# Moving the zeroing of one accumulator, grouping two more quads, and shifting two small steps in a graph-convolution kernel

## The chip, the cores and the metric

The kernel runs on one core of one Trainium2 chip. The metric is the device time of one execution in microseconds (us); before the change it was 2064.23 us, the median of three runs (2063.2 to 2068.42). A profiled execution of the same kernel took 2063.64 us.

## What is computed

A message-passing layer on 6250 nodes and 200000 edges, with the edges sorted by `dst`:

```python
h = jnp.maximum(_layernorm(x, axis=-1), 0.0)
xw = h @ W_in
W_ij = (shifted_softplus(f_ij @ W_f1 + b_f1) @ W_f2 + b_f2) * f_ij_cutoff
x_ij = xw[dst] * W_ij                          # one row of 128 for each edge
out = segment_sum(x_ij, src, num_segments=6250)
x = x + shifted_softplus(out @ W_o1 + b_o1) @ W_o2 + b_o2
```

The sum over `src`, which is in no order, is the hard part: every edge's row of 128 floats must be added to the row of its source node.

## The kernel before

**Chunks, quads and items.** 128 edges are a chunk and four chunks a quad; there are 1563 chunks and 391 quads. One long loop (`tile_gnn`, under `manual_schedule`) runs over items i = 0 to 398; item i starts the first matmul of quad i+1, the softplus of quad i, the second matmul of quad i-1, and so on. Whatever does not belong to every item is hung on a point of an item with `at(item, point, function)`. The points of one item follow each other in this order: L (loads), D0 and D1 (VectorE), A0 and A1 (ScalarE), DM and DR (VectorE), PE1 and PE2 (TensorE), A2 (ScalarE), D2 (VectorE), S (scatters). Each engine executes its own instructions in the order in which they were recorded, and so does each queue of DMA issues, SyncE's (SP) for all plain loads and stores in the loop and GpSimd's (POOL) for the scatters.

**How a quad's rows reach the sum.** There are two ways.

- A *plain* or *listed* quad is scattered: after pre-summing duplicates (plain: an equality matrix `eq` and four matmuls into `pp`, L547, copied to `s` by ScalarE, L555; listed: a list of duplicates worked out ahead) four indirect DMAs, one for each chunk, add its rows to an accumulator in DRAM (`scatter`, L597). There are four accumulators `acc0` to `acc3`, which the scatters take in turn: the first 140 scatters use three of them, later ones all four, and the last 64 leave out `acc0`, which is then read back (`r0_load`, `r0_tp`, `r0_add`, L1097) into the on-chip accumulator `accT`. A scatter waits until the one before it on the same accumulator has landed. The tile `s` has four buffers; each comes free when the scatters that read it have landed.
- A *grouped* quad is not scattered. A one-hot matrix `pm` (L677) permutes its rows by node group into 512 slots and 64 overflow slots; 16 matmuls (`pq`, L702) and 4 copies (L708) make four tiles `mst`. Eight grouped quads are a round. For each round four *units* (`unit_oh`, `unit_pe`, `unit_evac`) build one-hot matrices `so` (L780), multiply them with `mst` in 8 x 3 x 4 = 96 small matmuls into four PSUM banks `un` (L795), and add these to `accT` (L806). Overflow rows of two grouped quads share one scatter (`over_pe` to `over_scatter`, L715, L722, L742 to L769, index `oji`).

`sorted_quads` picks the grouped quads: from 8 on with gaps 2, 2, 2, 3, up to quad 390, cut to whole rounds. That gives 168 quads, the last one 383, in 21 rounds, and leaves 223 quads to be scattered, of which 192 are listed. All in all there are 987 scatters. `unit_slots` puts the last round's units on items 389, 391, 393 and 395; the last scatter, the overflow of quads 381 and 383, is due in item 394.

**Ranks.** Where a node's rows go in a permutation is worked out for eight quads at once: `rank_group` (VectorE, point D2, six items ahead of the round's first quad) makes the group one-hot `G` (L608 to L614) and then the counts and offsets `cnt`, `loc`, `ext` (L616 to L622); `rank_count` (TensorE, next item) uses `G`, `rank_own` and `rank_slot` the rest.

**Zeroing.** The accumulators are zeroed in ten DMAs of 320 KB each, from the first 640 columns of `accT`, which are set to zero at the start. `acc0` and `acc1` are zeroed through POOL's queue; `zero_piece` (L168) does `acc2` in items 0 to 4 and `acc3` in items 5, 7, ... 23 through SP's queue, between the loads.

**End.** Behind the loop a flag is read by all engines (would the rare slow path be needed? it is not taken with these inputs), all engines meet there, and the last stage begins: it loads `acc1` to `acc3` (L1378), adds them to `accT` and applies the last two matmuls, 13 groups of up to 512 nodes.

PSUM has four banks for all of `pp`, `pq`, `po`, `un`, `rtp` and other small results (tag B), and four for `z`, `xg` and `W`.

Of the kernel before, what the change touches and what calls it, by code (L numbers as in the profile page):

```python
# [26 lines left out]
SLOTS = GRP * CAP + OVC  # L27
MP0 = 8
MPGAPS = (2, 2, 2, 3)
MPEND = 0  # L30
RND = 8
EXTRA = 0
RKQ = 8
UOFF = (2, 6)
SW = 16
# [19 lines left out]
def tile_gnn(ctx: ExitStack, tc: tile.TileContext, x, fB, cT, srcT, srcr, dstr, win_, wf1, wf2, bias, bo1c, wo1,  # L55
# [3 lines left out]
    NP = x.shape[0]  # L59
# [15 lines left out]
    ACC_R = NP + P  # L75
    GN = NP // GRP
    ZR = 10 if ACC_R % 10 == 0 else 1
    ZL = 3
    K1_END, K2_END, K3_END = 2, 8, 140
    Z2, Z3 = [0,0,1,1,2,2,3,3,4,4], [5+2*j for j in range(10)]  # L80
    mpq = sorted_quads(NQ)
    mpi = {q: n for n, q in enumerate(mpq)}
    units = unit_its(mpq)
# [54 lines left out]
    wo1_sb = cp.tile([P, P], F32, name="wo1_sb")  # L138
    wo2_sb = cp.tile([P, P], F32, name="wo2_sb")
    accT = cp.tile([P, NP], F32, name="accT")  # L140
    zero = accT[:, :ACC_R // ZR]
    wgtb = cp.tile([P, 1], BF16, name="wgtb")
    iotw = cp.tile([P, GN // 2 + SLOTS], F16, name="iot")
    iot = iotw[:, GN // 2:]
# [455 lines left out]
    rk = {}  # L600
    mp = {}

    def rank_group(r):
        qs = mpq[RKQ * r:RKQ * r + RKQ]
        nc4 = 4 * len(qs)
        srcf = wk.tile([P, 4 * RKQ], F32, tag="srcf", name="srcf", bufs=1)
        o = 4 * (NS + RKQ * r)
        nc.vector.tensor_copy(srcf[:, :nc4], srcT_sb[:, o:o + nc4])  # L608
        srcf = srcf[:, :nc4]
        n = [P, nc4, GRP - 1]  # L610
        nc.vector.tensor_tensor(ge[:, :nc4, 1:GRP], srcf.unsqueeze(2).to_broadcast(n),
                                thr.unsqueeze(1).to_broadcast(n), op=ALU.is_ge)
        G = wk.tile([P, 4 * RKQ, GRP], BF16, tag="G", name="G", bufs=1)
        nc.vector.tensor_tensor(G[:, :nc4], ge[:, :nc4, :GRP], ge[:, :nc4, 1:], op=ALU.subtract)  # L614
        cnt = wk.tile([P, 4 * RKQ], F32, tag="cnt", name="cnt", bufs=1)
        nc.vector.tensor_reduce(cnt[:, :nc4], ge[:, :nc4, 1:GRP], axis=AX.X, op=ALU.add)  # L616
        loc = wk.tile([P, 4 * RKQ], F32, tag="loc", name="loc", bufs=1)
        nc.vector.scalar_tensor_tensor(loc[:, :nc4], cnt[:, :nc4], float(-GN), srcf, op0=ALU.mult, op1=ALU.add)
        ext = wk.tile([P, 4 * RKQ, 3], BF16, tag="ext", name="ext")
        nc.vector.memset(ext[:, :, 0], 0.0)  # L620
        nc.vector.tensor_scalar(ext[:, :nc4, 1], loc[:, :nc4], float(-(GN // 2)), None, op0=ALU.add)
        nc.vector.tensor_copy(ext[:, :nc4, 2], cnt[:, :nc4])  # L622
        rk[r] = {"G": G[:, :nc4], "cnt": cnt[:, :nc4], "ext": ext, "n": nc4, "qs": qs}

    def before_me(ps_t, src, w):
        n = src.shape[1]
# [79 lines left out]
    def perm_out(q, s):  # L706
        mp[q]["ms", s] = wk.tile([P, MW], BF16, tag=f"ms{s}", name="mst", bufs=RND + max(EXTRA, 2 * s))
        nc.scalar.copy(mp[q]["ms", s][:, :PW], mp[q].pop(("q", s))[:, :PW])  # L708
# [66 lines left out]
    def unit_oh(r, s, h):  # L775
        qs = round_quads(mpq, r)
        for q in qs[:len(qs) // 2] if h == 0 else qs[len(qs) // 2:]:
            so = wk.tile([P, GN], BF16, tag="so", name="so", bufs=RND + EXTRA)
            w = mp[q]["ms", s].bitcast(F32)
# [70 lines left out]
    with tc.manual_schedule():  # L850
# [26 lines left out]
        ext = cp.tile([HALF, 6], F32, name="ext")  # L877
# [86 lines left out]
        def at(i, point, fn, *a):  # L964
            hooks.setdefault((i, point), []).append((fn, a))
# [6 lines left out]
        if CE < EP // P:  # L972
            w = (CE + 4 * NS) // 2
# [131 lines left out]
        if spread:  # L1105
            k = clear(mid + 9, busy, 2)
# [3 lines left out]
            k = clear(NQ - 1, busy, 2)  # L1110
# [11 lines left out]
        for t in range(0, NPT, 4):  # L1122
            i = mid + 8 * (t // 4) if spread else 0
            at(min(i + 9, NQ + 1), "D2", x_bias, t)
        r0_at = 0
        for g in range(len(tgroups)):
            i = clear(max(r0_at + 1, ret_at + 5), units)
# [4 lines left out]
        for r in range(-(-len(mpq) // RKQ)):  # L1132
            i = mpq[RKQ * r]
            i = max(i, 6)
            at(i - 6, "D2", rank_group, r)
            at(i - 5, "PE2", rank_count, r)
            at(i - 4, "D0", rank_own, r)
            k = mpq[RKQ * r] if i == 6 else i - 2
            at(k, "PE2", rank_over, r)
            at(k + 1, "D0", rank_slot, r)  # L1140
# [3 lines left out]
        for w in range((LE - LB) // SW):  # L1144
            for g in range(4):
                n = LB + SW * (w - 1) + 4 * g
                i = splain[n] + 2 if w else 6 + 2 * g
                while w and (i - MP0) % sum(MPGAPS) not in UOFF:
                    i -= 1
                for k in range(2):  # L1150
                    kk = (LB + SW * w + 4 * g) // 2 + k
                    at(max(0, i + k - 2), "L", sb_load, kk)
                    at(i + k, "DM", l_eq, kk)
                i = clear(i + 2, units)
                at(i, "PE2", l_count, (LB + SW * w) // 4 + g)
                at(i + 1, "D0", l_dup, w, g)
            i += 1
            at(i, "D0", l_scan, w)
            i = clear(i, units)
            at(i, "PE2", l_before, w)  # L1160
            at(i + 1, "D0", l_index, w)
            assert i + 1 <= splain[LB + SW * w] + 1
            at(i + 2, "D2", l_id, w)
            i = clear(i + 3, units)
            at(i, "PE2", l_place, w)
            at(i + 1, "D0", l_take, w)
            i = clear(wend[w] + 12, units)
            at(i, "L", l_start, w)
            at(i, "A0", l_dg, w)
            at(i, "PE2", over_row, ("L", w))  # L1170
            at(i + 1, "D0", l_same, w)
            k = clear(i + 1, units)
            at(k - 1, "L", l_load, w)
            at(k, "PE2", l_sum, w)
            at(k + 1, "A0", l_copy, w)
            at(k + 1, "DM", l_ji, w)
            at(k + 1, "A2", over_int, ("L", w))
            at(k + 2, "S", over_scatter, ("L", w))
        if LE:
            for k in range(NACC):  # L1180
# [2 lines left out]
        for q in mpq:  # L1183
            at(q + 1, "D2", perm_oh, q)
            at(q + 2, "DR", part_rem, q, 1)
            at(q + 2, "DR", part_rem, q, 2)
            at(q + 2, "A2", part_ext, q)
            if q + 4 in units:
                for s in range(4):
                    at(q + 3, "PE2", permute, q, s)  # L1190
                for s in range(4):
                    at(q + 3, "PE2", perm_out, q, s)
            else:
                for s in range(4):
                    at(q + 3 + s // 2, "PE2", permute, q, s)
                    at(q + 4 + s // 2, "A0", perm_out, q, s)
            if mpi[q] % 2 or q == mpq[-1]:
                k = mpq[mpi[q] + 1] + 1 if mpi[q] + 1 < len(mpq) else q + 3
                at(k, "PE1", over_pe, q)
                at(k, "PE1", over_out, q)  # L1200
                at(q + 5, "DM", over_idx, q)
                at(q + 6, "A0", over_dg, q)
                k = clear(q + 6, units)
                at(k, "PE2", over_row, q)
                at(k + 1, "D0", over_eq, q)
                k = clear(q + 8, units)
                at(k, "PE2", over_sum, q)
                at(k + 1, "A0", over_copy, q)
                at(k + 1, "DM", over_ji, q)
                at(k + 1, "A2", over_int, q)  # L1210
                at(k + 2, "S", over_scatter, q)
        last = mpq[-1]
        for r in range(len(mpq) // RND):
# [263 lines left out]
def sorted_quads(nq):  # L1477
    qs, q = [], MP0
    while q < nq - MPEND:
        qs.append(q)  # L1480
        q += MPGAPS[(len(qs) - 1) % len(MPGAPS)]
    return qs if len(qs) % RND <= EXTRA else qs[:len(qs) // RND * RND]

# [23 lines left out]
def clear(i, busy, n=1):  # L1507
    while any(i + k in busy for k in range(n)):
        i += 1
    return i  # L1510
# [113 lines left out]
```

## Time and profile before

| | us |
|---|---|
| median of 3 runs (lowest, highest) | 2064.23 (2063.2, 2068.42) |
| profiled execution | 2063.64 |
| its span, first to last instruction | 2061.9 |
| TensorE (PE) busy | 1820.4 |
| GpSimd (POOL) busy | 1652.4 |
| VectorE (DVE) busy | 1650.9 |
| ScalarE (ACT) busy | 1470.8 |

The profile is of one execution. Times within it are counted from the first instruction. A line of the timeline gives start, duration, engine, line of the code, operation, tiles (out<-in) and count, and in brackets how long the engine was idle ahead of it and what ended that. A line of the table of stages gives the stretch, then busy time and count of each engine (or of one line alone), the granted TensorE clock, the busy share of the DMA engines and GB/s. In the groups of instructions, the numbers behind the first bar are busy time in us and mean duration of one in ns, and behind the second the idle time of the engine ahead of them.

### The profile page before, as it was taken

To read this page: it belongs to the slowest core of one execution; us is meant where nothing else is said; L and a number is where in the kernel's file an instruction comes from. 1 tells how busy PE (TensorE), PEld (TensorE's weight loads), DVE (VectorE), ACT (ScalarE), POOL (GpSimd) and SP (SyncE) were. 2 spreads that over 40 slices of the span, in tenths; PEclk is the share of its full clock that TensorE was granted. 3 is DMA by queue.
4 is the path that set the end of the run, shared out by engine and by line. 5 is a ranking of instruction groups with operands and counts; after the bars stand their busy time and mean duration, and the time that the engine had idled before them with its cause. 6 is when DMAs were issued, how large, how long until landed. Compare 5 with 4: busy or idle time off the path is not lost.

```text
span 2061.9 us, 54889 instructions
## 1 busy us (share of the span) xinstructions
PE 1820.4 (88%) x19121; PEld 1188.1 (58%) x19121; DVE 1650.9 (80%) x4449; ACT 1470.8 (71%) x3999; POOL 1652.4 (80%) x1040
## 2 busy tenths in 40 slices
PE   2578998899999999899989999999799899999966
PEld 1455555556655665565656566566565556666734
DVE  3577897798987988888888989888788687787745
ACT  2458776777777787777778787787677677788714
POOL 3578887888888888878788888888888888888884
PEclk9789999999999999999999999999999999999987
DMA  6887766667676776667666666766666666667647
GB/s 240 242 202 141 129 123 123 111 111 144 118 136 120 128 136 111 130 115 131 129 121 125 121 126 117 126 117 132 113 116 114 125 105 118 108 119 141 128 44 250
DMA packets 359675, 272.41 MB, mean 132 GB/s; under 512 B 97727, under 2 KB 319850, under 8 KB 359394
## 3 DMA queue, kind: packets, MB, share of 16 engines
q0 software_dynamic: 143728, 71.30, 34.4%
q1 hardware_dynamic: 215378, 197.50, 32.8%
q8 instruction: 151, 2.47, 0.5%
q14 instruction: 130, 1.06, 0.2%
q10 hardware_dynamic: 288, 0.07, 0.0%
HBM read 154.45 MB, written 114.24 MB: 130 GB/s over the span
## 4 chain that ended last, share of the span: by engine, by line
PE 46%; DVE 20%; ACT 10%; DMA 7%; issue 6%; POOL 5%; SPq 4%; DVEq 0%; ACTq 0%; POOLq 0%
PE pq L702 15%; PE W L520 10%; PE un L795 8%; POOL acc L597 5%; ACT xc L525 3%; PE po L715 2%; DVE accT L806 2%; DVE pt L691 2%; PE z L328 2%; ACT mst L708 2%; DVE eql L384 2%; PE xg L512 2%; DMA acc<-s,lji 2%; DVE pm L677 2%; ACT a L333 2%
## 5 line engine op out<-in xcount | busy, mean ns | idle before, releaser
L597 POOL DMA_INDIRECT acc<-s,lji x768 | 1254.4, 1633 | 250.4 <-issue 185.5
L702 PE MATMUL pq<-pt,pm 128*128 128x387 bf16 x2688 | 545.6, 346 | 43.2 <-ACT pt L697 10.6
L525 ACT ACTIVATE xc<-xg,cb 128x128 f32<-128x128 f32 x1564 | 448.0, 377 | 80.5 <-PE xg L512 73.4
L520 PE MATMUL W<-w,a 128*128 128x128 f32 x3128 | 467.7, 294 | 0.0
L520 PEld LDWEIGHTS W<-w,a 128*128 128x128 f32 x3128 | 392.2, 197 | 42.9 <-issue 4.5
L708 ACT CAST mst<-pq 128x387 bf16<-128x387 f32 x672 | 305.4, 481 | 149.7 <-PE pq L702 108.7
L702 PEld LDWEIGHTS <-pm 128*128 128x128 bf16 x2688 | 261.1, 100 | 235.6 <-issue 60.9
L795 PE MATMUL un<-so,mst 32*128 32x392 bf16 x8064 | 372.5, 327 | 11.9 <-ACT s L555 5.8
L795 PEld LDWEIGHTS <-mst 32*128 32x128 bf16 x8064 | 226.1, 93 | 152.0 <-issue 45.3
L338 ACT ACTIVATE a<-a,con 128x512 f32<-128x512 f32 x391 | 282.3, 722 | 12.7
L597 POOL DMA_INDIRECT acc<-s,ji x123 | 198.4, 1613 | 80.1 <-issue 26.7
L333 ACT ACTIVATE a<-z 128x512 f32<-128x512 f32 x391 | 238.0, 609 | 30.5 <-PE z L328 20.1
L691 DVE TENSOR_TENSOR pt<-pt 128x512 f32<-128x512 f32 x336 | 231.6, 689 | 5.8
L535 DVE TENSOR_TENSOR pt<-W,xc 128x512 f32<-128x512 f32 x168 | 115.5, 687 | 132.4 <-PE po L715 62.9
L677 DVE TENSOR_SCALAR pm<-iot,pos 128x576 bf16<-128x576 f16 x672 | 219.8, 388 | 0.0
L535 DVE TENSOR_TENSOR s<-W,xc 128x512 f32<-128x512 f32 x192 | 131.8, 686 | 75.7 <-ACT xc L525 44.6
L780 DVE TENSOR_SCALAR so<-iot,mst 128x392 bf16<-128x392 f16 x672 | 181.2, 333 | 9.7 <-PE un L795 9.2
L597 POOL DMA_INDIRECT acc<-os,oji x96 | 158.1, 1647 | 30.4 <-issue 18.3
L806 DVE TENSOR_TENSOR accT<-un,accT 128x392 f32<-128x392 f32 x320 | 158.4, 557 | 28.6 <-PE un L795 18.9
L512 PE MATMUL xg<-wn,oh 63*128 63x128 bf16 x1564 | 158.9, 224 | 25.0 <-DVE oh L345 13.8
L328 PE MATMUL z<-ft,ws 123*128 123x512 bf16 x391 | 151.7, 388 | 15.5 <-POOL b2rep L942 9.3
L509 PE MATMUL W<-b2rep,onesb 64*128 64x512 bf16 x391 | 155.6, 398 | 0.2 <-issue 0.2
(210 smaller groups left out, 1968.1 us busy)
## 6 DMA issues: line engine op xcount, KB each, us to landing
rb<-reld SPq DMA_DIRECT2D x391, 64.0 KB
fsd<-f SPq DMA_DIRECT2D x49, 480.0 KB
ft<-fsd SPq DMA_DIRECT2D x195, 120.0 KB
sb<-src SPq DMA_DIRECT2D x169, 128.0 KB
fb<-in_fB_dram SPq DMA_DIRECT2D x49, 320.0 KB
ft<-fsd SPq DMA_DIRECT2D x195, 80.0 KB
wn<-tab SPq DMA_DIRECT2D x782, 15.8 KB
acc<-s,lji POOLq DMA_INDIRECT x768
```

The source lines that it names most:

```text
L333: nc.scalar.activation(a, st[q]["z"], AF.Exp)
L338: nc.scalar.activation(a, a, AF.Ln, bias=half, scale=0.5)
L512: nc.tensor.matmul(xg[:, c, :], st[q]["oh"][a:a + NR, c * P:(c + 1) * P], wn[a:a + NR, c // 2, :], start=True, stop=True)
L520: nc.tensor.matmul(W[:, c, :], st[q]["a"][:, c * P:(c + 1) * P], w2, start=False, stop=(c == 3))
L525: nc.scalar.mul(xc[:, c, :], st[q]["xg"][:, c, :], late["c", q // CQ][:, 4 * (q % CQ) + c:4 * (q % CQ) + c + 1])
L535: nc.vector.tensor_tensor(m[:, :, :P], st[q]["W"], st[q]["xc"], op=ALU.mult)
L597: nc.gpsimd.indirect_dma_start(out=accs[k][:rows, :], out_offset=bass.IndirectOffsetOnAxis(ap=ji, axis=0), in_=s, in_offset=None, compute_ ...
L677: nc.vector.tensor_scalar(pm[:, c], iot[:, :SLOTS], rk[r]["pos"][:, 4 * j + c:4 * j + c + 1], None, op0=ALU.is_equal)
L691: nc.vector.tensor_tensor(pt[:, :, k * P:(k + 1) * P], a, high(a), op=ALU.subtract)
L702: nc.tensor.matmul(t[:, :PW], mp[q]["pm"][:, c, s * P:(s + 1) * P], high(mp[q]["pt"][:, c:c + 1, :PW])[:, 0], start=(c == 0), stop=(c == 3))
L708: nc.scalar.copy(mp[q]["ms", s][:, :PW], mp[q].pop(("q", s))[:, :PW])
L795: nc.tensor.matmul(ts[g][:, :GN], mp[q]["ms", s][v, k * P:(k + 1) * P], mp[q]["oh"][v], start=(q == qs[0] and k == 0), stop=(q == qs[-1] a ...
```

## The change

Four things change at once. `acc3` is zeroed in items 13, 16, ... 40, from the last 640 columns of `accT` (those of the first, which are overwritten earlier, could not serve so long). The list of grouped quads may run to 389 and may leave up to two quads over, which join the last round: quads 386 and 388 are now grouped, the last round has ten quads, the `so` tile ten buffers and the first `mst` tile ten, and the last units stand in items 394, 396, 398 and 400. The conversion of the overflow scatter's index to integers (`over_int`) moves from the end of ScalarE's work in one item to point A0 of the next, the scatter itself stays. The second half of `rank_group` becomes `rank_local`, one item later, behind it on VectorE.

With the two quads grouped, 221 quads are scattered, and there are 980 scatters. The last one, the overflow of quads 386 and 388, is due in item 399. `acc0` retires at scatter 916 and not 923, so its 13 groups are read back from item 375 on and not from 378.

```diff
 MPGAPS = (2, 2, 2, 3)
-MPEND = 0
+MPEND = 1
 RND = 8
-EXTRA = 0
+EXTRA = 2
...
-    Z2, Z3 = [0,0,1,1,2,2,3,3,4,4], [5+2*j for j in range(10)]
+    Z2, Z3 = [0, 0, 1, 1, 2, 2, 3, 3, 4, 4], range(13, 43, 3)
...
-    zero = accT[:, :ACC_R // ZR]
+    zero = accT[:, NP - ACC_R // ZR:]
...
         nc.vector.tensor_tensor(G[:, :nc4], ge[:, :nc4, :GRP], ge[:, :nc4, 1:], op=ALU.subtract)
+        rk[r] = {"G": G[:, :nc4], "n": nc4, "qs": qs, "srcf": srcf}
+
+    def rank_local(r):
+        nc4, srcf = rk[r]["n"], rk[r]["srcf"]
         cnt = wk.tile([P, 4 * RKQ], F32, tag="cnt", name="cnt", bufs=1)
...
-        rk[r] = {"G": G[:, :nc4], "cnt": cnt[:, :nc4], "ext": ext, "n": nc4, "qs": qs}
+        rk[r]["cnt"], rk[r]["ext"] = cnt[:, :nc4], ext
...
             at(i - 6, "D2", rank_group, r)
+            at(i - 5, "D2", rank_local, r)
             at(i - 5, "PE2", rank_count, r)
...
             at(k + 1, "DM", l_ji, w)
-            at(k + 1, "A2", over_int, ("L", w))
+            at(k + 2, "A0", over_int, ("L", w))
             at(k + 2, "S", over_scatter, ("L", w))
...
                 at(k + 1, "DM", over_ji, q)
-                at(k + 1, "A2", over_int, q)
+                at(k + 2, "A0", over_int, q)
                 at(k + 2, "S", over_scatter, q)
```

The functions that set the grouped quads and the units:

```python
def sorted_quads(nq):
    qs, q = [], MP0
    while q < nq - MPEND:
        qs.append(q)
        q += MPGAPS[(len(qs) - 1) % len(MPGAPS)]
    return qs if len(qs) % RND <= EXTRA else qs[:len(qs) // RND * RND]

def unit_slots(qs, r):
    if r == len(qs) // RND - 1:
        return [qs[-1] + 6 + 2 * s for s in range(4)]
```

## The prediction

> **What bounds the kernel now.** I read the page first, then the scatters' line by stages, then the end of POOL's, TensorE's and VectorE's timelines, then the start of POOL's and SP's. On the page no engine is full:
>
> ```profile
> PE 1820.4 (88%) x19121; PEld 1188.1 (58%) x19121; DVE 1650.9 (80%) x4449; ACT 1470.8 (71%) x3999; POOL 1652.4 (80%) x1040
> L597 POOL DMA_INDIRECT acc<-s,lji x768 | 1254.4, 1633 | 250.4 <-issue 185.5
> ```
>
> POOL at 80% looks idle, but its scatters (L597) are followed by 0.3 us of idle time that only "issue" ends. Here are two neighbours of the last stretch, and the table of stages for L597 alone:
>
> ```profile
> 1992.46 1.54 POOL L597 DMA_INDIRECT acc<-s,ji  x1 [0.30 <-issue]
> 1994.31 1.54 POOL L597 DMA_INDIRECT acc<-s,ji  x1 [0.31 <-issue]
> ...
> 2005.42 1.54 POOL L597 DMA_INDIRECT acc<-s,ji  x1 [0.31 <-issue]
> 2007.27 1.54 POOL L597 DMA_INDIRECT acc<-os,oji  x1 [0.30 <-issue]
> ```
>
> ```profile
> 58.00:200.00 142.00, 102.18 (x62) 0.84 0.81 195
> 200.00:860.00 660.00, 550.48 (x339) 0.97 0.68 125
> 860.00:1160.00 300.00, 244.73 (x150) 0.97 0.66 121
> 1160.00:1900.00 740.00, 623.75 (x382) 0.97 0.67 120
> ```
>
> The pitch of scatters with nothing in the way is 1994.31 - 1992.46 = 1.85 us. By stages it is 142/62 = 2.29, 660/339 = 1.95, 300/150 = 2.00 and 740/382 = 1.94 us. So from the first scatter at 58 us to the last at 2007 us POOL is the bound: it runs at its pitch, stretched most at the start, where the DMA engines are busiest (0.81), and a little between 860 and 1160 us, where five waits of POOL for rows exceed the 0.3 us, such as
>
> ```profile
> 997.25 1.74 POOL L597 DMA_INDIRECT acc<-s,lji  x1 [3.29 <-DVE s L535]
> ```
>
> In what order things end is shown by the chain (start, length, what) and by VectorE's last lines:
>
> ```profile
> 2007.27 3.23 DMA acc<-os,oji
> 2011.37 0.37 SPq L1378
> ```
>
> ```profile
> 1987.16 1.99 DVE L806 TENSOR_TENSOR accT<-un,accT 128x392 f32<-128x392 f32 x4 [1.52 <-PE un L795]
> 1996.72 1.98 DVE L806 TENSOR_TENSOR accT<-un,accT 128x392 f32<-128x392 f32 x4 [5.26 <-PE un L795]
> 1999.26 0.13 DVE L1289 TENSOR_SCALAR flagi<-flag 1x1 int32<-1x1 f32 x1
> ```
>
> The last scatter lands at 2010.50, and the first load of the last stage goes out 0.87 us later. VectorE's own work ended at 1999.4. The last stage then takes 2061.9 - 2011.4 = 50.5 us, which the change does not touch. So at the end POOL is 11 us behind the units.
>
> **Grouping two more quads: POOL.** 987 scatters become 980: eight of quads 386 and 388 go, one overflow scatter comes. At 1.85 us, the pitch of the stretch they leave, that is 7 x 1.85 = 13.0 us. The last scatter would start at 2007.27 - 13.0 = 1994.3 and land at 1997.5. Its index comes from matmuls that TensorE does behind the second unit, about 1986 by the sum below, so it isn't late.
>
> **Grouping two more quads: TensorE, and what is late next.** The units move behind quad 388's permutation, so their end has to be worked out anew.
>
> ```profile
> 1942.31 0.89 PE L715 MATMUL po<-pt,pm 128*64 128x387 bf16 x8
> 1949.09 1.56 PE L702 MATMUL pq<-pt,pm 128*128 128x387 bf16 x8
> 1950.59 0.39 PE L512 MATMUL xg<-wn,oh 63*128 63x128 bf16 x4
> 1953.88 1.16 PE L520 MATMUL W<-w,a 128*128 128x128 f32 x8
> 1954.87 0.38 PE L328 MATMUL z<-ft,ws 123*128 123x512 bf16 x1
> 1955.09 1.05 PE L547 MATMUL pp<-m,eq 128*128 128x129 f32 x8
> 1957.67 4.41 PE L795 MATMUL un<-so,mst 32*128 32x392 bf16 x94 [1.25 <-ACT s L555]
> 1972.23 7.19 PE L795 MATMUL un<-so,mst 32*128 32x392 bf16 x94 [4.50 <-ACT s L555]
> 1983.14 4.13 PE L795 MATMUL un<-so,mst 32*128 32x392 bf16 x93 [0.19 <-DVE accT L1097]
> 1991.01 5.81 PE L795 MATMUL un<-so,mst 32*128 32x392 bf16 x93 [1.49 <-DVE accT L1097]
> ```
>
> The last `z` starts at 1954.9 now, with TensorE busy without a break. Ahead of it the change puts three groups of `rtp` (four small matmuls each, costed at half a `pp`) and the rank matmuls of two quads (costed at one `pp`), and takes one `pp` out: an estimate of 3 x 0.5 + 1.05 - 1.05 = 1.5 us, so 1956.4. Behind it TensorE has, ahead of the first unit: three `pp` (3 x 1.05 = 3.2), two sets of `xg` and `W` (2 x 1.4 = 2.9), four batches of `pq` (4 x 1.4 = 5.7; a batch's 1.56 overlaps the next by some 0.1), one `po` (0.9) and small ones (1.0): 13.7 us, so the units start at about 1970.2. ScalarE's copies of `pp` no longer hold them up as they hold the second unit batch now (4.50 us): the buffers of `s` that quads 389 and 390 need were read by scatters of 382 and 384, the last of which is the 26th from the end now, so issued by 2007.27 - 25 x 1.85 = 1961.
>
> A unit has 120 matmuls in place of 96. The four batches above took 0.047, 0.076, 0.044 and 0.062 us for each matmul. The slow second one followed the 4.50 us wait, which goes; the other three together are 14.35/280 = 0.0512, so 6.15 us for 120. Then VectorE empties the four banks (1.99 us) before the next unit can start: a period of 8.2 us. Units start at 1970.2, 1978.4, 1986.6 and 1994.8; the last ends at 2001.0, its evacuation at 2003.0. Behind the last evacuation the flag's arithmetic took 0.7 us (1999.39 against 1998.70), which now comes ahead of it; reading the flag has no row of its own, and the meeting takes the 0.87 us from above. I take 2.0 for both, between 0.9 and 3. The last stage starts at 2005.0 and not 2011.4: **-6.4 us**, less than half of the 13.0, because the units are late next.
>
> Bounds: if all batches go at the fastest rate (4.13/93, so 5.3 us, period 7.4), the units end 3.3 us earlier and the gain is 9.7; if all go at the slowest (7.19/94, so 9.2 us, period 11.2), they end 12.2 us later and it is a loss of 5.8.
>
> [...]
>
> VectorE's and ScalarE's extra work for the two quads (`pm` four times 0.39, `pt` twice 0.69, copies of 0.48) lies beside TensorE's; without that cover it would be some 3 us.
>
> **Zeroing later.** No work is saved, ten DMAs of 320 KB stand elsewhere in SP's queue.
>
> ```profile
> L168 SPq DMA_DIRECT2D acc<-accT x20: 360/430/614, 45.9 to 173.4; - x20
> ```
>
> ```profile
> 106.26 0.46 SPq L168 DMA_DIRECT2D acc<-accT  x1
> ...
> 117.51 0.48 SPq L168 DMA_DIRECT2D acc<-accT  x1
> ...
> 130.06 0.48 SPq L168 DMA_DIRECT2D acc<-accT  x1
> ...
> 146.56 0.43 SPq L168 DMA_DIRECT2D acc<-accT  x1
> ```
>
> ```profile
> 111.98 1.64 POOL L597 DMA_INDIRECT acc<-s,ji  x1 [0.68 <-ACT xc L525]
> ...
> 123.57 1.77 POOL L597 DMA_INDIRECT acc<-s,ji  x1 [2.39 <-DMA acc<-s,ji]
> ...
> 135.79 1.54 POOL L597 DMA_INDIRECT acc<-s,ji  x1 [2.07 <-DMA acc<-s,ji]
> ...
> 152.94 1.54 POOL L597 DMA_INDIRECT acc<-s,ji  x1 [0.97 <-DMA acc<-s,ji]
> ```
>
> ```profile
> 80.00:120.00 40.00, 25.22 (x187) 18.93 (x188) 22.89 (x54) 19.76 (x58) 28.75 (x18) 0.74 0.88 227
> 220.00:240.00 20.00, 18.49 (x215) 12.16 (x212) 16.12 (x43) 15.75 (x47) 16.28 (x11) 1.00 0.72 135
> ```
>
> The fences show four pieces in SP's queue, the waits in POOL's, and all engines by stages (the last three columns: granted clock, DMA share, GB/s). About 6 us behind a piece's issue POOL waits: 0.7 us behind the piece at 106.3, 2.4 behind 117.5, 2.1 behind 130.1, 1.0 behind 146.6; the last three waits are for the landing of an earlier scatter. Four pieces (items 5 to 11) leave the stretch with a DMA share of 0.88, and as many more land where it is about 0.72. Above the usual 0.3 us, a piece costs between 0.4 (the wait of 0.68) and 2.1 us early, say 1.5, and 0.7 late: 4 x (1.5 - 0.7) = **-3 us**. Bounds: the stretch up to 200 us lies 142 - 62 x 1.95 = 21 us above the usual pitch; half of it, 10 us, is the most I give to four pieces, and if each late piece cost 0.7 and the early ones nothing, it is +3. The units of item 41 write over the zeros and so wait for the pieces of items 37 and 40; these are issued about the time of their items, near 255 us, and the unit's evacuation is due after 270, so I cost that wait at nothing; if it came, some 5 us of VectorE's time would lie behind POOL's backlog. `acc3`'s first scatter, number 144, starts at 364 us.
>
> **Rank preparation and late index.** Both add nothing and move work of VectorE and ScalarE that POOL's pace covers, except between 860 and 1160 us. One row each: the largest step that is moved, what ScalarE's conversion of the index waits for (us, times), what POOL's scatters wait for.
>
> ```profile
> L616 DVE TENSOR_REDUCE cnt<-ge 128x32 f32<-128x480 bf16 x21 | 13.4, 638 | 0.0
> ```
>
> ```profile
>   DMA acc<-os,oji: 35.5, 6
> ```
>
> ```profile
>   DVE s L535: 13.3, 12
> ```
>
> `rank_local` takes 0.64 us and four small steps, some 1.6 us, out of one item and puts it, once in 18 items, behind VectorE's work of the next, where the units of that place need no new one-hot but in the item after. ScalarE's six waits for a landing (35.5 us) are waits for POOL's own scatters, so they come where POOL is behind, and cutting them gains nothing; nor can the scatter come late, queued as it is behind four scatters of the same item (7.4 us). The gain is at most the 13.3 us of POOL's waits for rows; a loss as large as a third of that is possible if the order gets worse. I take -1, near the small end, since the split touches one item in 18.
>
> **The sum.** -6.4 - 3 - 1 = -10.4 us. The profiled execution took 2063.64, 0.6 below the median of 2064.23; so **2053.8** for the median.
>
> **The rivals.**
>
> - *Units at the full clock.* Waits of 2 us don't slow them; the tail gives 9.7: 2064.2 - 9.7 - 3 - 1 = 2050.5. For it: the 4.13 us batch; against it: the 5.81 us one. Chance 0.20. [...]
> - *Early waits go altogether.* The zeroing gives its bound of 10, the tail as forecast: 2064.2 - 6.4 - 10 - 1 = 2046.8. For it: the stage's pitch of 2.29 us; against: other loads fill the DMA engines there. Chance 0.10.
> - *Zeroing only moves its cost, and the units are slower.* All four batches' mean, 21.54/374 = 0.0576 a matmul, gives 6.9 us and a period of 9.0, so a tail gain of 3.4, and nothing else: 2060.8, no change to speak of. Chance 0.20.
> - *Units at half clock throughout: slower.* In the tail nothing else keeps TensorE busy; if every batch took 9.2 us, the units would end late enough to lose 5.8, and with the zeroing at its other bound of +3 it is 2073.0; alone it is 2070.0. It turns into a loss once a batch of 120 takes more than 7.8 us. Chance 0.08.
>
> That the change doesn't do what it says can be left out: the order of POOL's queue has seven scatters fewer at its end.
>
> **How the numbers follow.** The forecast has 0.42 and reaches from 2048 to 2060. A measurement of this kernel tells no less than about 0.3% (6.2 us) from no change, so faster means under 2058.0. Faster: 0.20 + 0.10 + 0.38 of the forecast = 0.68. Same: 0.04 of the forecast + 0.19 of the third rival = 0.23. Slower 0.09. The range 2044 to 2065 leaves out the half-clock rival, the far end of the early one and a little at the third's edge, under 0.2.
>
> **What would show it.** The last scatter's start: 11 us or more earlier, ahead of the units' last evacuation, if the two quads work as said; the units as the last thing before the last stage's loads; batches of 120 at 5.3, 6.2 or 9.2 us; the number of scatters up to 200 us, 62 now, at 63 or 64 if the zeroing helps; POOL's waits behind the new places of the pieces, 160 to 255 us, under 1 us each. The forecast is wrong if POOL still ends last, if the units start much after 1970 less what was won early, or if the middle of the kernel, 200 to 1900 us, changes its pitch by over 0.01 us (8 us over 870 scatters).

## The result, and the profile after the change

The changed kernel takes **2051.38 us** in the median of 20 runs (2045.38 to 2057.25), the kernel before 2063.41 (20 runs, 2055.3 to 2069.09). The ratio is 0.9945, 95% interval 0.9932 to 0.9958: 11.4 us faster, between 8.7 and 14.0. Forecast were 2053.8 us and a gain of 10.4. A second comparison gave 0.9957 (0.9942 to 0.9971). The profiled execution took 2047.98 us with a span of 2046.2, a favourable one: 15.7 us below the span of before, where the medians differ by 12.0.

The page of the changed kernel, engines and scatters, then its table of stages for the scatters alone:

```profile
PE 1828.6 (89%) x19254; PEld 1195.6 (58%) x19254; DVE 1658.5 (81%) x4486; ACT 1473.3 (72%) x4008; POOL 1639.4 (80%) x1033
...
L597 POOL DMA_INDIRECT acc<-s,lji x768 | 1251.2, 1629 | 247.3 <-issue 186.1
```

```profile
58.00:200.00 142.00, 102.64 (x63) 0.83 0.80 185
200.00:860.00 660.00, 546.69 (x335) 0.96 0.69 127
860.00:1160.00 300.00, 251.48 (x155) 0.97 0.67 122
1160.00:1900.00 740.00, 622.66 (x383) 0.98 0.67 122
```

TensorE has eight microseconds more work and POOL seven instructions fewer. By stages little moves: one scatter more up to 200 us, four fewer up to 860, five more (155, not 150) in the stretch where POOL had waited for rows, one more behind it.

The end is what the prediction was mostly about. TensorE's, VectorE's, POOL's and SP's lines there (start, length, engine, line, operation; L799 is the line of the units, L810 of their evacuation, L1383 of the last stage's loads). A unit's 120 matmuls show as a run of 117; three more start ahead of it, as the banks come free one by one:

```profile
1947.31 0.38 PE L328 MATMUL z<-ft,ws 123*128 123x512 bf16 x1
...
1961.58 5.13 PE L799 MATMUL un<-so,mst 32*128 32x392 bf16 x117
...
1970.19 6.81 PE L799 MATMUL un<-so,mst 32*128 32x392 bf16 x117 [1.24 <-DVE oeq L751]
...
1979.46 5.13 PE L799 MATMUL un<-so,mst 32*128 32x392 bf16 x117 [0.15 <-DVE accT L810]
...
1987.02 6.81 PE L799 MATMUL un<-so,mst 32*128 32x392 bf16 x117 [0.15 <-DVE accT L810]
```

```profile
1993.72 1.99 DVE L810 TENSOR_TENSOR accT<-un,accT 128x392 f32<-128x392 f32 x4 [5.60 <-PE un L799]
```

```profile
1989.38 1.54 POOL L597 DMA_INDIRECT acc<-os,oji  x1 [0.30 <-DMA acc<-s,ji]
```

```profile
1996.41 20.44 SPq L1383 DMA_DIRECT2D ta_in<-acc  x30
```

The last scatter starts at 1989.4 and, at the 3.2 to 3.4 us that the last scatters of these profiles take to land, is done by 1992.8; the last evacuation ends at 1995.7, and the last stage's loads go out 0.7 us later. In this profile the units end last and no longer POOL. From the last `z` to those loads it takes 1996.4 - 1947.3 = 49.1 us, where it took 2011.4 - 1954.9 = 56.5.

### The profile page after: what moved, and what is told of

The parts are those of the page before. It is cut to its first block, busy times and chain, and to the rows that moved or that the text cites. A ratio compares the mean times of both kernels' runs of the same rounds, so it can differ in the third digit from the quotient of the medians.

```text
span 2046.2 us, 55192 instructions
## 1 busy us (share of the span) xinstructions
PE 1828.6 (89%) x19254; PEld 1195.6 (58%) x19254; DVE 1658.5 (81%) x4486; ACT 1473.3 (72%) x4008; POOL 1639.4 (80%) x1033
## 5 line engine op out<-in xcount | busy, mean ns | idle before, releaser
L799 PE MATMUL un<-so,mst 32*128 32x392 bf16 x8160 | 374.4, 327 | 7.3 <-DVE accT L810 1.8
L799 PEld LDWEIGHTS <-mst 32*128 32x128 bf16 x8160 | 228.3, 93 | 147.1 <-issue 38.9
L597 POOL DMA_INDIRECT acc<-s,ji x115 | 187.3, 1629 | 77.6 <-issue 24.9
L810 DVE TENSOR_TENSOR accT<-un,accT 128x392 f32<-128x392 f32 x320 | 158.5, 557 | 30.3 <-PE un L799 18.3
```

Source lines behind the costliest of these rows:

```text
L597: nc.gpsimd.indirect_dma_start(out=accs[k][:rows, :], out_offset=bass.IndirectOffsetOnAxis(ap=ji, axis=0), in_=s, in_offset=None, compute_ ...
L799: nc.tensor.matmul(ts[g][:, :GN], mp[q]["ms", s][v, k * P:(k + 1) * P], mp[q]["oh"][v], start=(q == qs[0] and k == 0), stop=(q == qs[-1] a ...
```

## The experiments

All comparisons are with the kernel before on the same chip, as ratios with a 95% interval; microseconds are the ratio times the median of before in that comparison. One profile of a kernel lies some microseconds to either side of its median, so places are read from profiles and prices from the medians.

### Each part alone

**The two quads grouped** (`MPEND = 1`, `EXTRA = 2`, nothing else).

> Only the two more grouped quads and the last round of ten. Theory A (the tail is the gain): 980 scatters; the last scatter lands 5 us or so ahead of the last unit's evacuation, the last stage's loads go out some 49 us behind the last z matmul and not 56.5; 6 to 8 us less than before, ratio about 0.9966. Theory B (the gain of the whole change comes from the middle of the kernel): 3 us or less here. POOL's scatters up to number 900 start when they did, within the 4 us by which single runs differ.

Measured: 2056.39 against 2067.13 us, ratio 0.9957 (0.9938 to 0.9976): 8.9 us faster (5.0 to 12.8). Its TensorE, VectorE, POOL and SP lines, and the last scatter's landing as the chain of its profile has it:

```profile
1959.57 0.38 PE L328 MATMUL z<-ft,ws 123*128 123x512 bf16 x1
...
1982.48 5.13 PE L795 MATMUL un<-so,mst 32*128 32x392 bf16 x117 [1.27 <-DVE oeq L747]
...
1996.59 5.13 PE L795 MATMUL un<-so,mst 32*128 32x392 bf16 x117
```

```profile
2001.91 1.98 DVE L806 TENSOR_TENSOR accT<-un,accT 128x392 f32<-128x392 f32 x4 [4.22 <-PE un L795]
```

```profile
2000.57 1.54 POOL L597 DMA_INDIRECT acc<-os,oji  x1 [0.31 <-DMA acc<-s,ji]
```

```profile
2000.57 3.33 DMA acc<-os,oji
```

```profile
2004.69 15.49 SPq L1378 DMA_DIRECT2D ta_in<-acc  x24
```

Here the two ends meet: the last evacuation ends at 2003.9, the last scatter lands at 2003.9, and the loads go out 0.8 us later; the chain goes through the scatter. The units' batches all take 5.13 us, and the stretch from `z` to the loads is 2004.7 - 1959.6 = 45.1 us.

**The zeroing later** (`Z3 = range(13, 43, 3)` and the zeros from the last columns of `accT`).

> Only the zeroing of the fourth accumulator in items 13 to 40, from the last columns. Theory A as predicted: 3 us less, 64 scatters up to 200 us. Theory B, from the two profiles (scatter 60 is 2 us earlier after the change, scatter 130 is 4 us later): the early gain of 2 us is given back with 2 to 6 us more between 210 and 360 us, and the run is 0 to 4 us longer than before.

Measured: 2067.26 against 2067.13 us, ratio 1.0004 (0.9984 to 1.0024): +0.8 us, between -3.3 and +5.0. No gain is shown.

**The rank preparation in two pieces** (`rank_local` one item behind `rank_group`).

> Only the rank preparation in two pieces. Theory A as predicted: 1 us less, within noise. Theory B: the waits of POOL for rows between 860 and 1160 us go (five waits, 9.7 us above the usual 0.3 us), and the run is 5 to 9 us shorter, with POOL's pitch in that stage 1.94 and not 2.00 us.

Measured: 2062.37 against 2067.13 us, ratio 0.9972 (0.9952 to 0.9993): 5.8 us faster (1.4 to 9.9). The gain is the size that theory B named, but not at its place: between 860 and 1160 us this kernel's profile has 149 scatters, a pitch of 2.01 us, and the waits for rows are 12.1 us in all, where they were 13.3.

**The late index** (`over_int` at point A0 of the next item).

> Only the conversion of the overflow index to integers in the next item. Theory A as predicted: no change, within 2 us; ScalarE's waits for the landing of an earlier overflow scatter (35.5 us, six times) shrink to some 20 us with no effect on POOL. Theory B: those waits hold TensorE up where POOL is not behind, and the run is 3 to 6 us shorter.

Measured: 2065.98 against 2067.13 us, ratio 0.9991 (0.9973 to 1.0009): -1.9 us, between -5.6 and +1.9. What the conversion waits for, in the kernel before (us, times) and then in this one:

```profile
  DVE ojd L765: 21.9, 22
```

```profile
  DMA acc<-os,oji: 28.4, 5
  DVE ojd L765: 4.3, 5
```

The step does take ScalarE's waits for VectorE's `ojd` away, 21.9 us down to 4.3. The waits for a landing stay (35.5 before, 28.4 now). For the time alone it isn't shown to matter.

**Rank preparation and index together.**

> The kernel before with the rank preparation in two pieces and the later index, without the other two parts. Theory A (each does what it did alone, the two add up): 5.8 + 1.9 = 7.7 us less, ratio 0.996. Theory B (the split's gain alone was the noise of its own runs; as predicted the two are worth 1 us): 0 to 2 us less. In the profile by A POOL's waits between scatters 400 and 550 are shorter than the 9.7 us of before; by B they stay.

Measured: 2060.07 against 2067.49 us, ratio 0.9963 (0.9945 to 0.9981): 7.6 us faster (3.9 to 11.4). With the grouping's 8.9 that makes 16.5, more than the whole change brings.

### The zeroing again

**The changed kernel with the old zeroing** (`Z3 = [5+2*j for j in range(10)]`, zeros from the first columns).

> The changed kernel with the fourth accumulator zeroed in items 5 to 23 from the first columns, as before; the other three parts stay. By the prediction's term the later zeroing was worth 3 us, so this would be 3 us longer than the changed kernel, 8 us under before. By the theory that zeroing gives nothing or costs a little between 200 and 360 us, it is as fast as the changed kernel or up to 4 us faster: 11 to 15 us under before, with scatters 61 to 150 at a pitch of 2.02 and not 2.08 us.

Measured: 2051.06 against 2067.49 us, ratio 0.9919 (0.9893 to 0.9944): 16.7 us faster (11.6 to 22.1).

**The changed kernel once more**, to have it beside others:

> The changed kernel once more, so that it stands beside the next three on one chip: 11 to 12 us under before, ratio 0.9945.

Measured: 2050.89 against 2060.48 us, ratio 0.9957 (0.9942 to 0.9971): 8.9 us faster (6.0 to 11.9). The end of its profile differs from that of the first one:

```profile
1992.57 1.98 DVE L810 TENSOR_TENSOR accT<-un,accT 128x392 f32<-128x392 f32 x4 [3.92 <-PE un L799]
```

```profile
1991.52 3.43 DMA acc<-os,oji
```

```profile
1995.75 19.69 SPq L1383 DMA_DIRECT2D ta_in<-acc  x30
```

All four batches took 5.13 us, the last evacuation ended at 1994.6, and the last scatter landed 0.4 us behind it, at 1995.0. Here POOL ends last, narrowly. So which of the two ends last in the changed kernel depends on the execution.

**Each piece of zeroing issued twice**, the second time into a spare tensor that nothing reads, once at the old places and once at the new ones:

```diff
+    accs.append(dp.tile([ACC_R + LR, P], F32, name="spare"))
...
+            at(Z3[j] if spread else 0, "L", zero_piece, nc.sync, 4, j)
```

> The kernel before, with a second DMA behind each of the ten zeroing pieces of items 5 to 23, of the same size, into a spare DRAM tensor: what ten pieces cost early. By the prediction (a piece costs 1.5 us up to item 11 and 0.7 later) 4 x 1.5 + 6 x 0.7 = 10 us longer than before, by the theory that POOL's early waits have other causes 0 to 4 us.

> The kernel with the later zeroing alone, with a second DMA behind each piece, in items 13 to 40: what ten pieces cost late. By the prediction 10 x 0.7 = 7 us longer than the later zeroing alone, which took as long as before. If a late piece costs more than an early one, as POOL's pitch between scatters 61 and 150 hints (2.06 and 2.08 us against 2.02), this is longer than the kernel with doubled early pieces.

Measured: early 2064.19 against 2060.48 us, ratio 1.0020 (1.0004 to 1.0036), 4.1 us for ten pieces (0.8 to 7.4), so 0.4 us a piece; late 2061.5, ratio 1.0006 (0.9990 to 1.0022), 1.2 us (-2.1 to 4.5), so 0.1 a piece. Both are against the kernel before; the later zeroing alone, in its own comparison, had taken +0.8.

The prediction had read POOL's waits at 112 to 153 us as the price of early pieces, since each stood some 6 us behind one. In the changed kernel the first piece of `acc3` goes out at 125.8 us. POOL's lines of the stretch ahead of it, then the zeroing's line with those who waited for it, and the line of another zeroing:

```profile
81.53 1.54 POOL L597 DMA_INDIRECT acc<-s,ji  x1 [1.75 <-DMA acc<-s,ji]
...
100.05 1.54 POOL L597 DMA_INDIRECT acc<-s,ji  x1 [1.66 <-DMA acc<-s,ji]
...
123.91 1.54 POOL L597 DMA_INDIRECT acc<-s,ji  x1 [1.26 <-DMA acc<-s,ji]
```

```profile
125.77 0.48 SPq L168 DMA_DIRECT2D acc<-accT  x1
```

```profile
L168 SPq DMA_DIRECT2D acc<-accT x20: 68/430/1498, 46.7 to 260.3; - x20
...
who waited for it (us, times):
  POOL acc L168: 3.8, 5
```

```profile
L173 SPq DMA_DIRECT2D acc<-accT x12: 422/474/1184, 50.8 to 124.8; - x12
```

Waits for landings of 1.3 to 1.8 us stand there without a piece of `acc3`, and between 110 and 155 us, where four pieces stood before and two stand now, POOL idles 5.0 us beyond its usual 0.3 us a scatter and idled 5.2 before. So most of these waits aren't the price of a piece. That doesn't clear zeroing as such: up to 77 us `acc2`'s pieces go out, and L173 (`zero_list`), which the description of the kernel leaves out, zeroes the lists' rows behind each accumulator in twelve DMAs of 256 KB through the same queue, nine of them between 79 and 125 us, in both kernels. What those cost was not tried. The last piece goes out at 260.3 us and no evacuation waits for it: only POOL's own zeroing of another accumulator is among the waiters.

### The units' wait for their banks

**The second and fourth unit of the last round in the other four PSUM banks, and the second half of the one-hots of all but the first unit an item earlier**, on top of the change:

```diff
-            t = ps.tile([P, 512], F32, tag="B", name="un", bufs=4)
+            t = ps.tile([P, 512], F32, tag="A" if r == len(mpq) // RND - 1 and s % 2 else "B", name="un", bufs=4)
...
-                at(k - 1, "D2", unit_oh, r, s, 1)
+                at(k - (2 if k > last and s else 1), "D2", unit_oh, r, s, 1)
```

> The changed kernel with the second and fourth unit of the last round in the four PSUM banks that z, xg and W leave free by then, and with their one-hot matrices made ahead of the evacuation, so that a unit needn't wait for the one before to be evacuated. Theory A (the units' evacuation and the clock are late next at the end): batches follow each other without the 2 us, TensorE keeps its full clock, all four are done 8 us earlier, and the last scatter, landing 3.8 us ahead of the last stage's loads now, sets the end: 3 us less than the changed kernel, 14 to 15 us under before. Theory B (the last scatter sets the end already): as the changed kernel.

Measured: 2049.53 against 2067.49 us, ratio 0.9912 (0.9886 to 0.9938): 18.2 us faster than before (12.8 to 23.6). Its TensorE, VectorE, POOL and SP lines at the end:

```profile
1974.17 10.11 PE L799 MATMUL un<-so,mst 32*128 32x392 bf16 x237 [0.43 <-ACT os L764]
```

```profile
1984.23 1.99 DVE L810 TENSOR_TENSOR accT<-un,accT 128x392 f32<-128x392 f32 x4 [2.35 <-PE un L799]
```

```profile
1989.26 1.54 POOL L597 DMA_INDIRECT acc<-os,oji  x1 [0.30 <-DMA acc<-s,ji]
```

```profile
1993.31 19.81 SPq L1383 DMA_DIRECT2D ta_in<-acc  x30
```

Without the wait for the banks TensorE does the third and fourth unit in one run, the last evacuation ends at 1986.2, 9.5 us earlier than in the changed kernel, and POOL's last scatter, at the same place as in the changed kernel's first profile (1989.3 and 1989.4), ends last again. So the loads move from 1996.4 to 1993.3, by 3.1 us and not by 9.5. In that execution of the changed kernel the units ended last, and by this much; in the second one there was nothing to win.

**The same with the old zeroing**, the best that the parts pointed to:

> Three of the four parts (not the later zeroing), and the units of the last round in both halves of PSUM. If the later zeroing costs something, 3 to 4 us less than the changed kernel for the units and 0 to 4 us more for the zeroing: 15 to 19 us under before. If the later zeroing is worth the 3 us of the prediction, this is as fast as the changed kernel.

Measured: 2048.53 against 2060.48 us, ratio 0.9934 (0.9913 to 0.9955): 13.6 us faster (9.3 to 17.9); the change itself gave 8.9 in the same comparison, with intervals that overlap. Both kernels with the units in other banks are faster than the kernel before and have the largest gain of their comparison; which of the two zeroings suits them isn't told apart.

### What VectorE's burst costs

**The kernel before with the five short steps behind `G` issued twice**, the second time into spare tiles:

```diff
+        cnt2 = wk.tile([P, 4 * RKQ], F32, tag="cnt2", name="cnt2", bufs=1)
+        nc.vector.tensor_reduce(cnt2[:, :nc4], ge[:, :nc4, 1:GRP], axis=AX.X, op=ALU.add)
...
+        nc.vector.tensor_copy(ext2[:, :nc4, 2], cnt2[:, :nc4])
```

> The kernel before, with the five short VectorE steps that make the rank's count, place and offset (six instructions, about 1.6 us for a group) issued a second time into spare tiles, right behind the first, for each rank group. Theory A (VectorE's burst of work in that item is what the split of the rank preparation relieves, so more burst costs): about 5 us over the kernel before, a ratio near 1.0025, and the last z matmul later by about as much. Theory B (the gain of the split alone does not come from the length of that burst): 0 to 1 us, a ratio of 1.000 within its interval. A ratio under 0.999 would speak against both.

Measured: 2082.64 against 2068.62 us, ratio **1.0078** (1.0050 to 1.0105): 16 us slower (10 to 22), three times what the theory that blamed the burst had expected and far from the other one. (The records show five added instructions a group, 105 in 21 groups.) The page, and what the scatters wait for:

```profile
PE 1822.4 (88%) x19121; PEld 1191.2 (57%) x19121; DVE 1672.4 (80%) x4554; ACT 1471.5 (71%) x3999; POOL 1660.8 (80%) x1040
...
L597 POOL DMA_INDIRECT acc<-s,lji x768 | 1265.6, 1648 | 256.8 <-issue 180.3
```

```profile
  DVE s L535: 21.3, 18
```

VectorE is busy 1672.4 - 1650.9 = 21.5 us longer, about 1.0 us a group, and 16 of it come out in the time. The span of the profile grew by 2078.9 - 2061.9 = 17.0 us. POOL shows it as waits for rows that grow from 13.3 us to 21.3 and as 1660.8 - 1652.4 = 8.4 us more of busy time.

Where it happens is seen in the starts of the `z` matmuls, one for each quad. The doubled steps run between the `z` of the quad four ahead of a round's first one and the `z` of the next quad (in 19 or 20 of 21 rounds), and the stretch that grows is the next one, up to the `z` of the quad two ahead. The kernel before and this one, sums of that next stretch over 20 rounds, all but the first (length, then busy time of each engine, then means of one stretch):

```profile
sum 115.41, PE 111.35 PEld 65.39 DVE 107.50 ACT 77.47 POOL 95.12; mean PE 5.57 PEld 3.27 DVE 5.37 ACT 3.87 POOL 4.76
```

```profile
sum 132.98, PE 118.31 PEld 68.09 DVE 126.76 ACT 78.46 POOL 109.33; mean PE 5.92 PEld 3.40 DVE 6.34 ACT 3.92 POOL 5.47
```

These 20 stretches alone are 17.6 us longer, so about the whole cost arises there. Before, TensorE and VectorE are both nearly full in them, idle for 4.1 and 7.9 us of 115.4. Now VectorE is idle for 6.2 of 133.0, while TensorE's idle time grows to 14.7 and POOL's from 20.3 to 23.7: VectorE, with the work that the doubled steps have pushed back, sets the pace in these stretches, though over the whole span it is busy for 80%. So VectorE's work at this place isn't covered by POOL's pace.

POOL's scatters of listed quads last 1648 ns in place of 1633. All 987 together took 1619.3 us, 8.4 more, little beyond the 1607.5 to 1616.7 of the seven other kernels with as many. The scatters beside an added step aren't longer: the 35 that overlap one last 1.62 us in the mean, the other 952 1.64.

Does the split relieve the same thing? The waits for rows (us, times) in the changed kernel, in the one with the split alone, in the changed one with the old zeroing, and in the one with doubled late pieces, which has no split:

```profile
  DVE s L535: 5.1, 10
```

```profile
  DVE s L535: 12.1, 9
```

```profile
  DVE s L535: 15.9, 13
```

```profile
  DVE s L536: 4.2, 8
```

The row, which the prediction had taken as the bound of the gain, says nothing of the split: it lies on both sides of the 13.3 of before with it and without it. The `z` matmuls tell more. In the six kernels with neither split nor doubled steps the stretch in which the rank preparation ends takes 5.26 to 5.40 us in the mean of 20 rounds and the next one 5.77 to 5.84; in the seven with the split it is 4.86 to 5.04 and 5.93 to 6.09. Both together are 11.13 and 10.94 us in the mean, so 0.19 x 20 = 3.8 us of gain sit in these two stretches, within the 1.4 to 9.9 measured.

## Why the prediction was right, and where it was not

**The total** came out 1 us (by the ratio) to 2.4 us (by the medians) from the forecast, through terms of which one was right within its interval and two were off in opposite directions. That it came so near is luck.

**What bounds the kernel: half right.** POOL does end last before the change, and seven scatters fewer do bring its end to that of the units. But "work of VectorE and ScalarE that POOL's pace covers" failed: 21.5 us more of VectorE's work cost 16 us. The prediction took the pitch of the scatters for the bound and didn't use the chain on the page of before, in which POOL has 5%:

```profile
PE 46%; DVE 20%; ACT 10%; DMA 7%; issue 6%; POOL 5%; SPq 4%; DVEq 0%; ACTq 0%; POOLq 0%
```

**Grouping: the mechanism right in part, the size within its interval.** Forecast -6.4, measured -8.9 (5.0 to 12.8 faster). "The units are late next" holds in some executions. The four profiles with the units as changed (landings of the first and third at 3.3 us, an estimate from the others' 3.2 to 3.4):

| | batches at 6.81 us | last evacuation ends | last scatter lands | loads go out | `z` to loads |
|---|---|---|---|---|---|
| changed kernel | 2 of 4 | 1995.7 | 1992.7 | 1996.4 | 49.1 |
| changed kernel once more | none | 1994.6 | 1995.0 | 1995.8 | 45.2 |
| with the old zeroing | 1 of 4 | 2000.8 | 1999.2 | 2001.5 | 46.5 |
| grouping alone | none | 2003.9 | 2003.9 | 2004.7 | 45.1 |

The forecast had 2005.0 - 1956.4 = 48.6 us from `z` to the loads and the units 2003.0 - 1997.5 = 5.5 us behind POOL. Where a batch is slow the units do end last, by 3.0 and 1.6 us; where none is, both end within 0.4 us. In the changed kernel the units started 13.6 us behind `z` (13.7 forecast). The batches were mis-sized: not 6.15 us for 120 but, in the run of 117, 13 times 5.13 and 3 times 6.81. The rival of units at full clock is what two of these executions did, with four batches of 5.13 us each (in the kernel with the grouping alone at a granted clock of 1.00), and its 9.7 is nearer to the 8.9 than the forecast's 6.4.

**Zeroing later: the step failed.** The term of -3 rested on waits "about 6 us behind a piece's issue", and POOL's waits in that stretch stay as long with half of the pieces gone. Measured alone it is +0.8 (-3.3 to +5.0); the changed kernel against the one with the old zeroing (two comparisons, -11.4 and -8.9 against -16.7) speaks for a loss of 5 to 8, the kernel with its units in other banks and the best one (-18.2 against -13.6) for a gain of 5, neither pair within one comparison. Doubling the early pieces cost 0.4 us each (0.1 to 0.7), the lowest of the prices that the prediction had read (0.4 to 2.1), and the late ones 0.1 (-0.2 to 0.5): so some 3 us were to be had by these prices, and the direct comparison doesn't show them. Its sign stays open. That no evacuation would wait for the last pieces was right.

**Rank preparation and index: the term was mis-sized.** Forecast -1 together, measured -7.6 (3.9 to 11.4 faster), -5.8 (1.4 to 9.9) for the split alone. The prediction had capped it by POOL's waits for rows, 13.3 us, and taken the small end "since the split touches one item in 18". That burst falls where VectorE is nearly full: doubling 1.0 us of it cost 0.77 us a group in the mean (16.1/21), and moving it into the next item brought 5.8/21 = 0.28. The late index did cut ScalarE's waits, by 17.6 us of those for `ojd`, and alone moved the time by nothing that can be told.

**The sum of the parts.** -8.9 - 7.6 + 0.8 = -15.7, against -11.4 and -8.9 for the whole. The parts' intervals add up to some 7 us either way, so this is no contradiction, but it may hide a cost of the later zeroing beside the other parts.

**What stays open.** Whether zeroing late is a small gain or a small loss, and what the twelve smaller zeroings cost. Why the parts add up to more than the whole, if they do.

## What to carry to other kernels

An engine that looked like the bound on average didn't cover another engine's burst here: 21.5 us more of VectorE's work cost 16. Before costing moved work at nothing, double it in place and see what it costs, and where. A wait that follows a transfer in time needn't be its price (waits of 1.3 to 1.8 us stood here without a piece): double the transfer, and look for the wait where the transfer is absent, with nothing like it left there. Where a queue's end is cut, work out what ends next and when: here the units came level with POOL, and gave back up to some 3 us of the cut where their batches were slow.

## What the runs showed of the hardware

The units' slow batches aren't slow by their work. Stages of the changed kernel and of the kernel with the grouping alone (stretch and length, TensorE's busy time and count, granted clock, DMA share, GB/s), first a fast and a slow batch of the changed kernel, then stretches of 3.4 us, the length of the one at half the clock (the changed kernel's last ends with its batch), of the changed kernel and of the other:

```profile
1961.60:1966.70 5.10, 5.10 (x117) 1.00 0.43 41
1970.20:1977.00 6.80, 6.80 (x117) 0.75 0.41 37
```

```profile
1967.40:1970.80 3.40, 1.88 (x21) 1.00 0.37 40
1970.80:1974.20 3.40, 3.40 (x49) 0.50 0.42 39
1974.20:1977.00 2.80, 2.80 (x65) 1.00 0.49 44
```

```profile
1977.60:1981.00 3.40, 2.52 (x38) 1.00 0.46 43
1981.00:1984.40 3.40, 2.13 (x49) 1.00 0.34 26
1984.40:1987.80 3.40, 3.21 (x77) 1.00 0.37 34
```

The granted clock was 1.00 over the fast batch and 0.75 over the slow one, but not evenly: in the slow batch it was 0.50 for one stretch of 3.4 us and 1.00 behind it, which loses 1.7 us. In the 3.4 us ahead of that stretch TensorE was busy for 1.88 us (0.55). In the kernel with the grouping alone the pause was 1.27 us, as long as the 1.24 in the changed kernel; in the three stretches around it TensorE was busy for 2.52, 2.13 and 3.21 us, and the clock stayed at 1.00. So here 3.4 us with 0.55 of the time busy were followed by half the clock and 3.4 us with 0.63 weren't; what made the difference wasn't tried by itself. In the kernel before, the batches of 7.19, 4.13 and 5.81 us were granted 0.59, 1.00 and 0.70. With no wait between the third and the fourth unit, 237 matmuls ran in 10.11 us, 0.043 us each, where the fast batch's took 5.13/117 = 0.044, so without a slow stretch.
